# Gathering 1.1 million table rows: no two-SBUF operations on VectorE, one tile of each block by SyncE

## The chip, the core and the metric

The kernel runs on one core of a Trainium2 chip. A core has five engines that work side by side: TensorE (PE, matrix products, results in PSUM), VectorE (DVE), ScalarE (ACT), GpSimd (POOL) and SyncE (SP). In this kernel GpSimd issues the indirect DMAs, each of which fetches 128 rows of a table by 128 ids; SyncE issues ordinary DMAs. The metric is the time of one execution in device microseconds (us); smaller is better.

## What is computed

For each of 16384 samples there are 69 ids of one user and one label id, all rows of a table `emb` with 96 columns. Each user row is weighed by a small network that also sees the label's row, the weighted rows are summed in 10 groups of fields, and three dense layers give one number.

```python
u  = emb[batch_user]                       # 16384 x 69 x 96
ql = emb[batch_label[:, 0]]                # 16384 x 96
q  = broadcast(ql)
z  = concatenate([q, u, q - u, q * u])     # 384 wide
h  = dice(z @ W1 + b1, a1)                 # 64 wide
att = (h @ W2 + b2) @ W3 + b3              # 1 wide
pre = where(batch_user < ITEM_NUM, u * att, 0)    # ITEM_NUM = 100000
pooled = einsum('gf,bfe->bge', window, pre)       # 10 groups of fields
x = concatenate([pooled, ql])              # 1056 wide
h = dice(bn(x @ Wf1 + bf1), af1)           # 200 wide
h = dice(bn(h @ Wf2 + bf2), af2)           # 80 wide
out = h @ Wf3 + bf3
# bn(x) = x / sqrt(1 + eps);  dice(x, a) = (a * (1 - p) + p) * x,  p = sigmoid(bn(x))
```

## The kernel before

A block has 512 samples, and there are 32 blocks. The first 64 fields of a block form 64 "main chunks" of 512 rows (8 samples x 64 fields), the last 5 fields form 5 "tail chunks" (one field, 512 samples): 69 chunks, 276 gathers of 128 rows. Chunks are handled in pairs, one pair a step, 1104 steps in all, software-pipelined: a step gathers and turns pair i, computes the hidden layer of pair i-2 and pools pair i-8.

```python
def map_ids(n, ids):                       # ids of ITEM_NUM go to a row of zeros behind the table
    rows = ipool.tile([P, NT], I32, tag="rows", name=f"rows{n}")
    nc.vector.scalar_tensor_tensor(rows, ids[:, 0:NT], float(ITEM_NUM), ids[:, 0:NT],
                                   ALU.is_ge, ALU.add)                              # L110
    return rows

def head_gather(n, part):                  # 32 label rows of block n, by SyncE
    ...
    _, at = nc.values_load_multi_w_load_instructions(                               # L252
        lab[n : n + 1, part * NLD : (part + 1) * NLD],      # lab lies in HBM
        engines=[mybir.EngineType.SP], ...)
    for i, row in enumerate(at):
        nc.sync.dma_start(out=qs[n][p + i : p + i + 1, k, :], in_=emb[bass.ds(row, 1), :])  # L260

def fetch(i):                              # one pair of chunks
    ...
            for t in range(4):
                gather(u[:, 4 * j + t, :], rows[n][:, 4 * k + t : 4 * k + t + 1])   # L229, GpSimd
                nc.tensor.transpose(ptr[:, t * P : (t + 1) * P], u[:, 4 * j + t, :], ident)  # L325
    ...                                    # then q * u on VectorE (L328), a copy on ScalarE (L336)

def hidden(i, ph, uT, quT):                # four products into ph (L343), sigmoid, dice
    ...
    nc.vector.tensor_mul(y, ph, y)         # L347, ph in PSUM

def spread(b, row):                        # attention weights times the window of groups
    ...
    nc.vector.tensor_scalar(w, pt[...], bb, None, ALU.add)                          # L373
    nc.vector.tensor_tensor(rw..., R..., w..., ALU.mult)    # L376: R and w both in SBUF
    return rw

def pool(i, u, rw):                        # 4 products a chunk, two records each (L393)
    ...

def top1(n, h, part, p1):                  # first dense layer, 100 of its 200 outputs
    ...                                    # 16 products into p1, four in a step     L423
    nc.vector.tensor_scalar(x1, p1, S_BN, sbf1[h], ALU.mult, ALU.add)               # L427
    nc.scalar.activation(g1, x1, AF.Sigmoid, scale=S_DICE)
    nc.scalar.activation(g1, g1, AF.Identity, bias=af1c[h], scale=naf1c[h])
    nc.vector.tensor_mul(x1, x1, g1)       # L430: both in SBUF

def top2(n): ...                           # the same with 80 outputs; L438 and L441
def top3(n, x2): ...                       # one output; stored by SyncE at L449
```

The buffers `u` of the gathered rows are 14 pairs deep. In each block's 34.5 steps SyncE fetches 16 parts of 32 label rows for the block to come, the ids of a block (140 KB), and stores one block's results.

Of the kernel before, what the change touches and what calls it, by code (L numbers as in the profile page):

```python
# [53 lines left out]
NCOL = NT + NQ  # L54
NLD = 32
NPAIR = NBLK * NCH // 2
# [5 lines left out]


@with_exitstack
def rec_kernel(
# [3 lines left out]
    lab: bass.AP,  # L69
    emb: bass.AP,  # L70
    W1: bass.AP,
# [28 lines left out]
    xpool = ctx.enter_context(tc.tile_pool(name="xpool", bufs=1))  # L100

# [5 lines left out]
    def map_ids(n, ids):  # L107

        rows = ipool.tile([P, NT], I32, tag="rows", name=f"rows{n}")
        nc.vector.scalar_tensor_tensor(rows, ids[:, 0:NT], float(ITEM_NUM), ids[:, 0:NT], ALU.is_ge, ALU.add)  # L110
        return rows

    ids, rows = {0: load_ids(0)}, {}
    rows[0] = map_ids(0, ids[0])
# [74 lines left out]
    naf1c = [one_minus(t, f"naf1c{i}") for i, t in enumerate(af1c)]  # L189
    naf2c = one_minus(af2c, "naf2c")  # L190
    sbf1 = []
    for i in range(2):
        t = const.tile([DH, 1], F32, name=f"sbf1_{i}")
        nc.vector.tensor_scalar_mul(t, bf1c[i], S_BN)
        sbf1.append(t)
    sbf2 = const.tile([D2, 1], F32, name="sbf2")
    nc.vector.tensor_scalar_mul(sbf2, bf2c, S_BN)
# [30 lines left out]
    def gather(dst, index):  # L228
        nc.gpsimd.indirect_dma_start(  # L229
            out=dst,  # L230
            out_offset=None,
            in_=emb,
            in_offset=bass.IndirectOffsetOnAxis(ap=index, axis=0),
        )

    def chunk(c):

        return divmod(c, NCH)

    def first_head():  # L240

        q = bpool.tile([P, NQ, E], F32, tag="q", name="q0")
        for k in range(NQ):
            gather(q[:, k, :], ids[0][:, NT + k : NT + k + 1])
        return q

    def head_gather(n, part):

        if part == 0:
            qs[n] = bpool.tile([P, NQ, E], F32, tag="q", name=f"q{n}")  # L250
        k, p = divmod(part * NLD, P)
        _, at = nc.values_load_multi_w_load_instructions(  # L252
            lab[n : n + 1, part * NLD : (part + 1) * NLD],
            engines=[mybir.EngineType.SP],
            min_val=0,
            max_val=ITEM_NUM,
            skip_runtime_bounds_check_because="labels are rows of the table",
        )
        for i, row in enumerate(at):
            nc.sync.dma_start(out=qs[n][p + i : p + i + 1, k, :], in_=emb[bass.ds(row, 1), :])  # L260
# [31 lines left out]
    def seed(i):  # L292

        ph = ps_h.tile([P, 512], F32, tag="h", name=f"ph{i}")
        nc.tensor.matmul(ph, zrow[:, 0:P], zrow, start=True, stop=False)  # L295
        (n0, k0), (n1, k1) = chunk(2 * i), chunk(2 * i + 1)
        if n0 == n1 and k1 < NMAIN:
            nc.scalar.copy(  # L298
                ph.rearrange("h (s f) -> h s f", f=FM), by_field(cs[n0][0][:, k0 * NS : (k0 + 1) * NS])
            )  # L300
        elif n0 == n1 and k0 >= NMAIN:
            nc.scalar.copy(ph, cs[n0][1])
        else:
            for j, (n, k) in enumerate([(n0, k0), (n1, k1)]):
                lo, hi = j * H1, (j + 1) * H1
                if k < NMAIN:
                    nc.scalar.copy(
                        ph[lo:hi].rearrange("h (s f) -> h s f", f=FM),
                        by_field(cs[n][1][lo:hi, k * NS : (k + 1) * NS]),
                    )  # L310
                else:
                    nc.scalar.copy(ph[lo:hi], cs[n][1][lo:hi, :])
        return ph

    def fetch(i):

        u = upool.tile([P, 8, E], F32, tag="u", name=f"u{i}")
        uT = tpool.tile([E, 2, 512], F32, tag="uT", name=f"uT{i}")
        quT = tpool.tile([E, 2, 512], F32, tag="quT", name=f"quT{i}")
        for j in range(2):  # L320
            n, k = chunk(2 * i + j)
            ptr = ps_tr.tile([E, 512], F32, tag="tr", name=f"ptr{i}_{j}")
            for t in range(4):
                gather(u[:, 4 * j + t, :], rows[n][:, 4 * k + t : 4 * k + t + 1])
                nc.tensor.transpose(ptr[:, t * P : (t + 1) * P], u[:, 4 * j + t, :], ident)  # L325
            q = qTs[n % 2][0:E]
            if k < NMAIN:
                nc.vector.tensor_tensor(  # L328
                    quT[:, j, :].rearrange("e (s f) -> e s f", f=FM),
                    ptr.rearrange("e (s f) -> e s f", f=FM),  # L330
                    by_field(q[:, k * NS : (k + 1) * NS]),
                    ALU.mult,
                )
            else:
                nc.vector.tensor_tensor(quT[:, j, :], ptr, q[:, 0:BLK], ALU.mult)
            nc.scalar.copy(uT[:, j, :], ptr)  # L336
        return u, uT, quT
# [28 lines left out]
    def spread(b, row):  # L366

        pt = ps_x.tile([P, 4, 4, 32], F32, tag="x", name=f"patt{b}")
        for t in range(4):
            nc.tensor.transpose(pt[:, t].rearrange("p k j -> p (k j)"), row[:, t * P : (t + 1) * P], ident)  # L370
        rw = rpool.tile([P, 4, 2, 4, 2 * G], F32, tag="rw", name=f"rw{b}")
        w = rpool.tile([P, 4, 2, 4], F32, tag="w", name=f"w{b}")
        nc.vector.tensor_scalar(  # L373
            w, pt[:, :, :, 0:2].rearrange("p t k j -> p k j t"), bb, None, ALU.add
        )
        nc.vector.tensor_tensor(  # L376
            rw.rearrange("p k j t g -> p (k j t) g"),
            R.rearrange("p (k g) -> p k g", k=1).to_broadcast([P, 32, 2 * G]),
            w.rearrange("p k j (t o) -> p (k j t) o", o=1).to_broadcast([P, 32, 2 * G]),
            ALU.mult,  # L380
        )
        return rw

    def pool(i, u, rw):
# [6 lines left out]
        for j, n, k in todo:  # L391
            for t in range(4):
                nc.tensor.matmul(  # L393
                    pa[:, j, 2 * t : 2 * t + 2, :].rearrange("e n g -> e (n g)"),
                    u[:, 4 * j + t, :],
                    rw[:, i % 4, j, t, :],
# [14 lines left out]

    KTOP = G + 1 + NTAIL

    def top1(n, h, part, p1):

        if part == 0:
            p1 = ps_m.tile([DH, BLK], F32, tag="m", name=f"p1_{n}_{h}")
        for k in range(part * KTOP // 4, (part + 1) * KTOP // 4):
            if k <= G:
                w, x = wf1[:, k], pooled[n][:, k, :] if k < G else qTs[n % 2][0:E, 0:BLK]  # L420
            else:
                w, x = V[:, k - G - 1], pres[n][:, k - G - 1, :]
# [3 lines left out]
        x1, g1 = x1s[n][:, h, :], xpool.tile([DH, BLK], F32, tag="g1", name=f"g1_{n}_{h}")  # L426
        nc.vector.tensor_scalar(x1, p1, S_BN, sbf1[h], ALU.mult, ALU.add)  # L427
        nc.scalar.activation(g1, x1, AF.Sigmoid, scale=S_DICE)
        nc.scalar.activation(g1, g1, AF.Identity, bias=af1c[h], scale=naf1c[h])
        nc.vector.tensor_mul(x1, x1, g1)  # L430

    def top2(n):
        x2 = xpool.tile([D2, BLK], F32, tag="x2", name=f"x2_{n}")
        g2 = xpool.tile([DH, BLK], F32, tag="g1", name=f"g2_{n}")[0:D2]
        p2 = ps_m.tile([D2, BLK], F32, tag="m", name=f"p2_{n}")
        for i in range(2):
            nc.tensor.matmul(p2, wf2[:, i, :], x1s[n][:, i, :], start=(i == 0), stop=(i == 1))
        nc.vector.tensor_scalar(x2, p2, S_BN, sbf2, ALU.mult, ALU.add)  # L438
        nc.scalar.activation(g2, x2, AF.Sigmoid, scale=S_DICE)
        nc.scalar.activation(g2, g2, AF.Identity, bias=af2c, scale=naf2c)  # L440
        nc.vector.tensor_mul(x2, x2, g2)  # L441
        return x2

    def top3(n, x2):
        p3 = ps_m.tile([1, BLK], F32, tag="m", name=f"p3_{n}")
        nc.tensor.matmul(p3, wf3, x2, start=True, stop=True)
        res = xpool.tile([1, BLK], F32, tag="res", name=f"res{n}")
        nc.vector.tensor_scalar(res, p3, bf3c, None, ALU.add)
        nc.sync.dma_start(out=out_v[n : n + 1], in_=res)  # L449
# [3 lines left out]
    cs, pooled, pres, x1s, x2s, qs, us, hs, phs, ys, bands, rws, p1s = ({} for _ in range(13))  # L453

    def top_steps(n):


        def half(h, part):
            if h == 0 and part == 0:
                x1s[n] = xpool.tile([DH, 2, BLK], F32, tag="x1", name=f"x1_{n}")  # L460
            p1s[n] = top1(n, h, part, p1s.get(n))

        steps = [lambda h=h, part=part: half(h, part) for h in range(2) for part in range(4)]
        steps.append(lambda: x2s.__setitem__(n, top2(n)))
        steps.append(lambda: top3(n, x2s.pop(n)))
# [8 lines left out]
    for n in range(NBLK):  # L474
        first, end = n * NCH // 2, ((n + 1) * NCH - 1) // 2
        if n > 0:
            at(first - 24, lambda n=n: ids.__setitem__(n, load_ids(n)))
            at(first - 21, lambda n=n: rows.__setitem__(n, map_ids(n, ids[n])))
            for part in range(BLK // NLD):
                at(first - 31 + part, lambda n=n, part=part: head_gather(n, part))  # L480
            at(first - 11, lambda n=n: head_turn(n, qs.pop(n)))
            at(first - 9, lambda n=n: cs.__setitem__(n, head_row(n)))
        for s, work in enumerate(top_steps(n)):
            at(end + POOL_LAG + 4 + s, work)
# [3 lines left out]
    with tc.manual_schedule():  # L488
        head_turn(0, first_head())
        cs[0] = head_row(0)  # L490
        for i in range(NPAIR + POOL_LAG + 16):
            if 0 <= i - 1 < NPAIR:
                phs[i - 1] = seed(i - 1)
            if 0 <= i - POOL_LAG < NPAIR:
                k = i - POOL_LAG
                pool(k, us.pop(k), rws[k // 4])
                if k % 4 == 3:
                    rws.pop(k // 4)
# [14 lines left out]
            if 0 <= i - 2 < NPAIR:  # L513
                ys[i - 2] = hidden(i - 2, phs.pop(i - 2), *hs[i - 2])
            if i < NPAIR:
# [58 lines left out]
```

## Time and profile before

| | |
|---|---|
| time, median of 3 | 15474.4 us (15444.3 to 15497.4) |
| the profiled execution | 11178.9 us, span 11177.1 |
| PE busy | 9700.5 us (87%), granted clock 0.707 on average |
| ACT busy | 3760.0 us (34%) |
| DVE busy | 3187.3 us (29%) |
| POOL busy | 8404.8 us (75%) |
| DMA | 456.8 MB moved, 41 GB/s |

The profiled execution is shorter than the timed ones. All that a view of the profile says holds for the profiled execution.

How to read the views: a group's line gives source line, engine, operation, tiles (out<-in), the count, then busy time and the mean of one instruction in ns, then the idle time of the engine just before these instructions and what ended most of it. A line of the waits reads "engine, tile, line <- what it waited for: us in total, times, longest". "Issue" is idle time in which the engine waited for nothing that the profile shows. A line of the timeline begins with the start and the length in us. A row of digits cuts the span in 40 slices, in tenths of it; PEclk is the clock that was granted to TensorE.

### The profile page before, as it was taken

Reading aid. Unit: us, or ns where it says so; the run is one execution under the profiler, and the core shown is the slowest. Engines: PE = TensorE matmul, PEld = TensorE weight load, DVE = VectorE, ACT = ScalarE, POOL = GpSimd, SP = SyncE. Lnnn points to the kernel's source line nnn. Section 1 sums busy time; section 2 is a strip of 40 time slices with the busy share of each in tenths; the row PEclk is TensorE's granted clock in tenths of the full one; section 3 lists DMA queues with packets and bytes.
Section 4 is the critical chain, followed back from the end, with each engine's and each line's share of the span. In section 5 each row is a group of like instructions: output and inputs, shape, how many; then the busy total and the mean of one; then the engine's idle time right before and its main releaser. Section 6 shows DMA issues by size and latency. Waiting matters only on the chain.

```text
span 11177.1 us, 157529 instructions
## 1 busy us (share of the span) xinstructions
PE 9700.5 (87%) x41348; PEld 4721.0 (42%) x41348; DVE 3187.3 (29%) x5424; ACT 3760.0 (34%) x6086; POOL 8404.8 (75%) x8842
## 2 busy tenths in 40 slices
PE   6888888888888898888888888888888888988888
PEld 3444444444444444444444444444444344444444
DVE  2222222222222222222222222222222222222222
ACT  2333333333333333333333333333333333333332
POOL 7777777777777777777777777777777777777775
PEclk6767677677776767767777667776677776677767
DMA  2222222222222222222222222222222222222221
GB/s 45 41 41 41 41 41 41 41 41 41 41 41 41 41 41 41 41 42 41 41 41 41 41 41 41 40 41 42 41 41 41 41 42 41 41 41 41 41 40 29
DMA packets 323169, 456.81 MB, mean 41 GB/s; under 512 B 175712, under 2 KB 180864, under 8 KB 322272
## 3 DMA queue, kind: packets, MB, share of 16 engines
q0 software_dynamic: 282752, 434.87, 19.6%
q1 hardware_dynamic: 37886, 10.92, 0.5%
q8 instruction: 333, 5.46, 0.2%
q14 instruction: 564, 4.62, 0.1%
q10 hardware_dynamic: 1634, 0.94, 0.0%
HBM read 446.04 MB, written 0.07 MB: 40 GB/s over the span
## 4 chain that ended last, share of the span: by engine, by line
PE 33%; POOL 32%; issue 16%; DMA 10%; SPq 5%; ACT 2%; DVE 1%; POOLq 0%; ACTq 0%
POOL u L229 32%; PE ph L343 12%; DMA u<-in_emb,rows 10%; PE acc L393 9%; PE p L423 4%; SPq L260 3%; PE ptr L325 3%; PE prow L354 2%; SPq L252 2%; PE ph L295 2%; PE pa L363 1%; ACT y L346 1%; DVE y L347 1%; ACT y L345 1%; PE patt L370 1%
## 5 line engine op out<-in xcount | busy, mean ns | idle before, releaser
L229 POOL DMA_INDIRECT u<-in_emb,rows x8832 | 8400.1, 951 | 2692.9 <-issue 2459.0
L325 PE MATMUL ptr<-ident,u 128*96 128x128 f32 x8832 | 2006.4, 353 | 1189.5 <-DMA u<-in_emb,rows 1172.1
L325 PEld LDWEIGHTS ptr<-ident,u 128*96 128x96 f32 x8832 | 1221.0, 155 | 3053.7 <-DMA u<-in_emb,rows 1526.9
L393 PEld LDWEIGHTS acc<-rw,u 128*96 128x96 f32 x16384 | 2048.5, 217 | 531.8 <-issue 531.2
L393 PE MATMUL acc<-rw,u 128*96 128x20 f32 x16384 | 2160.4, 282 | 1.8 <-DVE rw L376 1.3
L336 ACT COPY uT<-ptr 96x512 f32<-96x512 f32 x2208 | 1283.4, 581 | 2207.0 <-DVE quT L328 2039.4
L347 DVE TENSOR_TENSOR y<-ph,y 128x512 f32<-128x512 f32 x1104 | 763.5, 692 | 4394.8 <-ACT y L346 4292.3
L345 ACT ACTIVATE y<-ph 128x512 f32<-128x512 f32 x1104 | 659.1, 597 | 3754.1 <-PE ph L343 3753.9
L343 PE MATMUL ph<-uT,A 96*64 96x512 f32 x4416 | 1793.5, 904 | 0.0
L343 PE MATMUL ph<-quT,w 96*64 96x512 f32 x4416 | 1671.9, 847 | 0.0
L328 DVE TENSOR_TENSOR quT<-ptr,qT 96x512 f32<-96x512 f32 x2048 | 1348.9, 679 | 611.5 <-PE ptr L325 607.0
L402 DVE COPY pooled<-acc 96x160 f32<-96x160 f32 x1008 | 433.3, 430 | 2189.9 <-PE acc L393 2184.4
L346 ACT ACTIVATE y<-y,a1c,na1c 128x512 f32<-128x512 f32 x1104 | 897.2, 813 | 36.6
L343 PEld LDWEIGHTS ph<-quT,w 96*64 96x64 f32 x4416 | 442.8, 194 | 1074.9 <-issue 1074.9
L298 ACT COPY ph<-cT 128x512 f32<-128x512 f32 x1008 | 591.3, 587 | 498.2 <-PE ph L295 497.8
L295 PE MATMUL ph<-zrow 1*128 1x512 bf16 x1104 | 527.6, 478 | 193.4 <-DVE y L347 191.7
L423 PE MATMUL p<-pooled,wf 96*100 96x512 f32 x1280 | 659.4, 660 | 1.2 <-DVE x L427 0.8
L343 PEld LDWEIGHTS ph<-uT,A 96*64 96x64 f32 x4416 | 282.6, 177 | 550.0 <-issue 464.8
L354 PE MATMUL prow<-y,v 128*32 128x512 f32 x2208 | 455.2, 909 | 0.0
L356 ACT COPY row<-prow 128x512 f32<-128x512 f32 x276 | 161.5, 585 | 628.4 <-PE prow L354 622.9
L423 PEld LDWEIGHTS p<-pooled,wf 96*100 96x100 f32 x1280 | 232.2, 190 | 287.7 <-issue 285.5
L423 PE MATMUL p<-pre,V 96*100 96x512 f32 x640 | 314.6, 625 | 0.0
(71 smaller groups left out, 2318.5 us busy)
## 6 DMA issues: line engine op xcount, KB each, us to landing
q<-in_emb SPq DMA_DIRECT2D x15872, 0.4 KB
u<-in_emb,rows POOLq DMA_INDIRECT x8832
ids<-in_idx SPq DMA_DIRECT2D x32, 140.0 KB
wf<-in_Wf ACTq DMA_DIRECT2D x1, 825.0 KB
out<-res SPq DMA_DIRECT2D x32, 2.0 KB
w<-in_W SPq DMA_DIRECT2D x1, 96.0 KB
q<-in_emb,ids POOLq DMA_INDIRECT x4
wf<-in_Wf ACTq DMA_DIRECT2D x1, 62.5 KB
```

Of the source, the lines that this page charges most:

```text
L229: nc.gpsimd.indirect_dma_start(out=dst, out_offset=None, in_=emb, in_offset=bass.IndirectOffsetOnAxis(ap=index, axis=0),)
L295: nc.tensor.matmul(ph, zrow[:, 0:P], zrow, start=True, stop=False)
L325: nc.tensor.transpose(ptr[:, t * P : (t + 1) * P], u[:, 4 * j + t, :], ident)
L328: nc.vector.tensor_tensor(quT[:, j, :].rearrange("e (s f) -> e s f", f=FM), ptr.rearrange("e (s f) -> e s f", f=FM), by_field(q[:, k * NS ...
L336: nc.scalar.copy(uT[:, j, :], ptr)
L343: nc.tensor.matmul(ph[j * H1 : (j + 1) * H1, :], w, x[:, j, :], start=False, stop=last)
L345: nc.scalar.activation(y, ph, AF.Sigmoid, scale=S_DICE)
L346: nc.scalar.activation(y, y, AF.Identity, bias=a1c, scale=na1c)
L347: nc.vector.tensor_mul(y, ph, y)
L354: nc.tensor.matmul(pr[32 * k : 32 * (k + 1), :], v2, y, start=True, stop=True)
L393: nc.tensor.matmul(pa[:, j, 2 * t : 2 * t + 2, :].rearrange("e n g -> e (n g)"), u[:, 4 * j + t, :], rw[:, i % 4, j, t, :], start=True, st ...
L423: nc.tensor.matmul(p1, w[:, h * DH : (h + 1) * DH], x, start=(k == 0), stop=(k == KTOP - 1))
```

## The change

It has four parts:

- **No VectorE operation with two SBUF inputs.** The product with the window takes its weights from PSUM at once, in two operations instead of an addition and a product. The dense layers' dice does its scaling inside the sigmoid and multiplies straight from PSUM. The mapping of ids goes: the table of user rows is now one of its own, `rows`, whose last row is zero, so the ids are used as they are.
- **The last block in halves.** Its five tail chunks are taken before its last 16 main chunks, so that the dense layers of the first 256 samples can run before the last rows are there. Four poolings move one step earlier at the end.
- **Ids for SyncE's registers from SBUF.** They are loaded into a tile once per block, and registers are filled from it, instead of from HBM.
- **One more tile of rows per block through SyncE.** The first 128 rows of main chunk 8 (`SOLO`) of each block but the first come row by row from SyncE, like the labels, and not by a gather.

It is for GpSimd, which issues all gathers: one gather fewer in each block, and no VectorE operation with two SBUF inputs beside the others; for SyncE, which takes the tile over; and for the end of the run. The core of the diff:

```diff
+PARTS = P // NLD
+SOLO = 4 * 8
+EARLY = 3 * NMAIN // 4
...
-    rows[0] = map_ids(0, ids[0])
...
     def chunk(c):
-        return divmod(c, NCH)
+        n, k = divmod(c, NCH)
+        if n == NBLK - 1 and k >= EARLY:
+            k = NMAIN + k - EARLY if k < EARLY + NTAIL else k - NTAIL
+        return n, k
...
+    def load_solo(n):
+        t = spool.tile([(NQ + 1) * PARTS, NLD], I32, tag="sid", name=f"sid{n}")
+        nc.sync.dma_start(out=t, in_=solo[n : n + 1].rearrange("o p n -> (o p) n"))
+        return t
...
         _, at = nc.values_load_multi_w_load_instructions(
-            lab[n : n + 1, part * NLD : (part + 1) * NLD],
+            index,                                  # a row of the tile of load_solo
...
+    def solo_part(n, part):                         # parts 0-15: labels, 16-19: the solo tile
...
+                if n > 0 and 4 * k + t == SOLO:
+                    tiles.append(solos.pop(n))
+                else:
+                    tiles.append(u[:, 4 * j + t, :])
+                    gather(rows, tiles[-1], ids[n][:, 4 * k + t : 4 * k + t + 1])
...
-        nc.vector.tensor_scalar(w, pt[:, :, :, 0:2]..., bb, None, ALU.add)
-        nc.vector.tensor_tensor(rw..., R..., w..., ALU.mult)
+        for j in range(2):
+            nc.vector.scalar_tensor_tensor(rw[:, :, j, :], pt...[:, :, j : j + 1]..., bb, R...,
+                                           ALU.add, ALU.mult)
...
+    def dice(x, g, p, b, weights):
+        sb, sa, sna = weights
+        nc.scalar.activation(g, p, AF.Sigmoid, bias=sb, scale=S_BN * S_DICE)
+        nc.scalar.activation(g, g, AF.Identity, bias=sa, scale=sna)
+        nc.vector.scalar_tensor_tensor(x, p, b, g, ALU.add, ALU.mult)
...
-            for part in range(BLK // NLD):
-                at(first - 31 + part, lambda n=n, part=part: head_gather(n, part))
+            at(first - 33, lambda n=n: sids.__setitem__(n, load_solo(n)))
+            for part in range((NQ + 1) * PARTS):
+                at(first - 32 + part, lambda n=n, part=part: solo_part(n, part))
...
+        else:                                       # the last block
+            for s, work in enumerate(top_steps(n, slice(0, BLK // 2))):
+                at(NPAIR - 7 + s, work)
+            for s, work in enumerate(top_steps(n, slice(BLK // 2, BLK))):
+                at(end + POOL_LAG + 1 + s, work)
...
-        "emb": np.concatenate([x["emb"], np.zeros((1, E), np.float32)], axis=0),
+        "emb": x["emb"],
+        "rows": np.concatenate([x["emb"][:ITEM_NUM], np.zeros((1, E), np.float32)], axis=0),
```

## The prediction

> **What bounds the kernel now.** I read the engine totals first, then GpSimd's groups and waits, then single gathers. GpSimd does nothing but gathers, and its row shows how it spends the run:
>
> ```profile
> POOL 7777777777777777777777777777777777777775
> PEclk6767677677776767767777667776677776677767
> ...
> L229 POOL DMA_INDIRECT u<-in_emb,rows x8832 | 8400.1, 951 | 2692.9 <-issue 2459.0
> ...
> POOL u L229 <- issue: 2459.0, 8065, 0.3
> ...
> POOL u L229 <- PE ptr L325: 105.8, 347, 0.3
> ```
>
> GpSimd is 75% busy in every slice, and what is missing is not waiting. It stands idle 8065 times "for issue", 2459.0 us in total, which is 0.305 us each time and never over 0.3 as rounded. Waits put down to other engines have the same 0.3 as their longest, so they are that same gap under another name. The list of gather starts has no real hole anywhere: a gather of 128 rows begins every 1.249 us (0.944 by the median of one, 0.305 between two). With the 4 gathers of the first labels, 8836 x 1.249 = 11036 us; the first starts at 3.4 us and the last ends at 11101.3 us. So **the whole profiled span is one string of gathers**, with 62 us over, and a tail of 75.8 us behind the last.
>
> The other engines wait for it:
>
> ```profile
> PE ptr L325 <- DMA u<-in_emb,rows: 1172.1, 1424, 2.7
> ...
> SPq L449 <- DVE res L448: 2230.6, 31, 350.3
> ...
> 2006.70 13.11 SPq L260 DMA_DIRECT2D q<-in_emb  x32
> ```
>
> TensorE has 87% busy but waits 1172 us for gathered rows. SyncE, which fetches label rows one DMA each, waits 2230.6 us at the stores of results, so it has slack too: 20%.
>
> The 62 us over: the mean gather takes 951 ns, the median 944, so the total is 8400.1 - 8832 x 0.944 = 62.7 us too long. It is not spread evenly. Gathers of 1.2 to 1.6 us lie where VectorE works on two SBUF inputs:
>
> ```profile
> 11097.48 0.94 POOL L229 DMA_INDIRECT u<-in_emb,rows  x1 [0.30 <-issue]
> ...
> 11098.42 0.82 DVE L376 TENSOR_TENSOR rw<-R,w 128x640 f32<-128x640 f32 x1
> ...
> 11098.73 1.33 POOL L229 DMA_INDIRECT u<-in_emb,rows  x1 [0.30 <-issue]
> ...
> 11100.36 0.94 POOL L229 DMA_INDIRECT u<-in_emb,rows  x1 [0.30 <-issue]
> ```
>
> The product `rw = R * w` runs from 11098.42 to 11099.24; the gather that begins inside it takes 1.33 instead of 0.94 us. Pairing every gather over 0.96 us with what VectorE does in its time leaves only 5 without such a partner. By line, the excess over 0.943 us is 48.2 us for L376, 18.3 for L430, 2.3 for L441, 1.9 for L110 and 3.5 for the tail weights at the start.
>
> **The page and the times disagree.** The profiled execution took 11179 us, the timed ones 15474. No row of the page explains 4.3 ms. This is the largest uncertainty here, and I come back to it.
>
> [...]
>
> **The change, part by part, in the profiled execution.**
>
> 1. *One tile per block through SyncE.* Blocks 1 to 31 give up one gather each: 31 x 1.249 = **-39 us**. For this SyncE takes 20 parts of 32 rows per block instead of 16. A part costs 13.1 us of issues plus 4.9 us of register load (1.1 pointer, 3.4 values, 0.4 between), 18.0 us, so 16 parts take 288 of the 344 us that a block's 275 gathers last. With 20 parts at 18.0 it would be 360 us, and SyncE would set the pace.
> 2. *Ids from SBUF.* That is why this part is there. [...] SyncE stays under 344[...]. The solo tile is read some 15 steps (150 us) after its last row is issued. Also the first turned labels, for which TensorE waits 46 us once near the start, come earlier; GpSimd didn't feel that wait, so it is worth nothing.
> 3. *No two-SBUF operations.* The excess of L376, L430, L441 and L110 goes: 48.2 + 18.3 + 2.3 + 1.9 = 70.7 us; the tail weights keep theirs. Against the median instead of 0.943 it is some 8 us less. I take **-65 us**. What comes in instead reads PSUM as one input. VectorE loses 72 us (L427 and L438) it wasn't short of. ScalarE reads PSUM in the sigmoid at the same size, and the one PSUM buffer of the top layers is held about 2 us longer, in steps of 10 us; nothing on the path.
> 4. *Last block in halves.* After the last gather the chain now shows:
>
> ```profile
> 11132.79 17.26 PE p L423 x32
> 11150.08 0.76 DVE x L427
> 11150.88 13.99 PE p L423 x32
> ```
>
>    Half of the columns is done before the end: 31.3 us of products become about 15. The layers behind them (11164.9 to 11177.1) shrink by some 3 us with 256 columns. Before 11132.8 the last gather is followed by 8 pairs' poolings and the tail fields; four poolings of 1.5 to 2.8 us and two or three attention rows of 2 us move ahead of it: 8 to 12 us. Together **-30 us**, a tail of about 46.
>
> Sum: -39 - 65 - 30 = -134 us, a profiled span of about 11,043.
>
> **From there to the timed run.** Two readings. If the 4.3 ms are something that both kernels carry, the gain stays 134 us: 15,340. If the gathers themselves are slower when timed, (15474 - 76)/8836 = 1.743 us each, the first part grows to 31 x 1.743 = 54 us, the lock's to between 65 and 65 x 1.4 = 91, the tail's to 30 to 40: 150 to 185 us, or 15,290 to 15,325. I choose **15,325 us**, 1.0% less.
>
> **Rivals.**
>
> *SyncE becomes the bound.* For: it is the next busiest, with 128 more rows a block, 25%. If the timed run is slow because of SyncE, that is 483 us a block and 30 us a part instead of 18; were it the row issues, 20 such parts with a short load would take about 550 us a block, 17.6 ms. Against: its waits for results show 72 us of slack a block, and a row's data packet begins 0.85 us after its issue while eight semaphores in turn allow 8 x 0.41 = 3.3 us. If the slow thing were the register loads from HBM, the change would remove it and gain milliseconds. I give each of these 7 to 8%.
>
> *TensorE is the bound when timed.* With the clock at half throughout, start-to-start times in half-clock stretches add up to 10.7 us a pair of chunks, x 1104 = 11.8 ms. That is over 11.1 but far from 15.5, so the clock would have to be lower still than anything the profile shows. Then only the tail counts: 15,430.
>
> *The additional table costs.* The rows are now in HBM twice, 38 MB each. If the 4.3 ms had to do with the size of the inputs (44 MB before), the change would add nearly as much again, 19 ms. Nothing in the page speaks for it; 3%.
>
> *The lock is dearer than it looks.* All operations removed last 228.4 + 44.6 + 22.0 + 14.0 = 309 us. If a timed gather were held for the whole of each, 2% would be gained.
>
> **Range and chances.** The parts that I trust give 15,290 to 15,340; TensorE as the bound 15,430; the dearer lock 15,150. The range is 15,120 to 15,500, with the SyncE and table cases outside. 2% below is 15,165, 2% above 15,784. Faster by over 2%: 0.12 (dear lock, register loads). Slower by over 2%: 0.11 (SyncE, table). Within: 0.77.
>
> **What will show it.** Right: 8805 gathers at 1.249 us with no holes; gathers over 1.2 us nearly gone but for the first 150 us; last gather near 10,997; a tail of 40 to 50 us; SyncE still waiting at the store of results; register loads under 3 us. Wrong: GpSimd waiting for TensorE or for a solo tile (SyncE too slow), long gathers that stay beside PSUM operations (then it was not the second SBUF input), or a timed gain far from the profiled 134 us, which would mean that the two executions have different bounds.

## The result: 7.5% slower, and the profile after

The changed kernel took 16634.7 us (median of 4 runs, 16599.8 to 16664.8) against 15467.8 us before (median of 4, 15444.3 to 15497.4): a ratio of 1.0753, 95% interval 1.0721 to 1.0784. Predicted were 15,325 us and a range up to 15,500.

This time the page belongs to the times: the profiled execution of the changed kernel took 16615 us, and its span is 16613.2. First GpSimd's digits and group from the page of the changed kernel:

```profile
POOL 5444455444554445444455454554445544455444
...
L232 POOL DMA_INDIRECT u<-in_rows,ids x8801 | 8324.3, 946 | 8157.6 <-PE acc L416 4266.0
```

A gather takes 946 ns, as before (951), and there are the 31 fewer. But GpSimd is 50% busy instead of 75. It stands idle 8157.6 us, and what ends most of that is no longer "issue" but a product of TensorE (`acc`, the pooling, which gives a buffer of gathered rows free). Who holds TensorE, and what SyncE waits for, is in the waits of the changed kernel (us in total, times, longest):

```profile
POOL u L232 <- PE acc L416: 4266.0, 247, 104.6
...
PE pq L284 <- DMA q<-in_emb: 2918.1, 62, 62.2
...
SPq L473 <- DVE res L472: 485.7, 3, 284.5
```

TensorE waits 62 times, twice a block, for the label rows, which SyncE fetches. In the page of before the same wait was small:

```profile
PE pq L265 <- DMA q<-in_emb: 50.3, 24, 46.4
```

SyncE's wait at the stores of results has fallen from 2230.6 us in 31 stores to 485.7 in 3: in the other blocks SyncE comes to the store late. So the order of waiting has turned round: GpSimd waits for TensorE, TensorE for label rows, and SyncE for almost nothing. **SyncE sets the pace.**

Why it is so slow shows when its issues are laid beside what GpSimd does. Two stretches of the changed kernel's SyncE timeline (start, length, number of row issues; register loads are inside), and then the busy time by windows for the same stretches, whose pairs are PE, PEld, DVE, ACT and POOL:

```profile
1979.89 60.06 SPq L269 DMA_DIRECT2D q<-in_emb  x123
...
2098.81 78.56 SPq L269 DMA_DIRECT2D solo<-in_rows  x64
```

```profile
1980.00:2040.00 60.00, 0.42 (x1) 0.16 (x1) 0.00 (x0) 0.00 (x0) 0.00 (x0) 0.50 0.01 1
2099.00:2177.00 78.00, 46.79 (x193) 26.61 (x193) 13.13 (x24) 16.58 (x28) 50.59 (x55) 0.54 0.16 35
```

While GpSimd stands still (the fifth pair, 0.00 us), SyncE issues 123 rows in 60.06 us, 0.49 us each. Beside 55 gathers it needs 78.56 us for 64: 1.23 us each. Taken from one register load to the next, a part of 32 rows has a median of 15.6 us where no gather begins (157 parts) and of 30.3 us where gathers, at 1.249 us each, fill 80 to 95% of it (237 parts); the mean of all is 26.0 us. 20 such parts are 520 us a block, and 31 blocks 16.1 ms. In the page of before, a part cost 18.0 us beside gathers.

Where GpSimd stands, the other engines mostly stand too, so they could be what slows SyncE. The same trace tells them apart. Taken in groups of 8 rows without a register load between them, it has 98 groups in which no gather begins and TensorE begins at least one product a us: 0.41 us a row (median), as in the 497 groups where neither works. In 53 groups gathers begin and no product does: 1.09 us a row. SyncE's slowness goes with the gathers, not with TensorE.

### The profile page after: what moved, and what is told of

Same layout as the page of the kernel before. It is cut to its first block, busy times and chain, and to the rows that moved or that the text cites. A ratio compares the mean times of both kernels' runs of the same rounds, so it can differ in the third digit from the quotient of the medians.

```text
span 16613.2 us, 169743 instructions
## 1 busy us (share of the span) xinstructions
PE 9769.2 (59%) x41418; PEld 4967.8 (30%) x41418; DVE 3034.8 (18%) x5303; ACT 3745.8 (23%) x6092; POOL 8329.0 (50%) x8811
## 5 line engine op out<-in xcount | busy, mean ns | idle before, releaser
L232 POOL DMA_INDIRECT u<-in_rows,ids x8801 | 8324.3, 946 | 8157.6 <-PE acc L416 4266.0
L416 PEld LDWEIGHTS acc<-rw,u 128*96 128x96 f32 x16322 | 2147.8, 227 | 3562.8 <-issue 3556.7
L416 PE MATMUL acc<-rw,u 128*96 128x20 f32 x16322 | 2261.0, 290 | 4.3 <-DVE pooled L425 3.7
L367 PE MATMUL ph<-uT,A 96*64 96x512 f32 x4416 | 1877.8, 939 | 5.6 <-issue 5.4
L349 PE MATMUL ptr<-ident,u 128*96 128x128 f32 x8801 | 1713.3, 354 | 174.2 <-issue 140.3
L349 PEld LDWEIGHTS ptr<-ident,u 128*96 128x96 f32 x8801 | 1285.8, 164 | 1671.5 <-issue 1506.2
L367 PE MATMUL ph<-quT,w 96*64 96x512 f32 x4416 | 1782.0, 895 | 2.0 <-issue 1.8
L284 PE MATMUL pq<-ident,q 128*96 128x128 f32 x128 | 42.6, 381 | 2918.3 <-DMA q<-in_emb 2918.1
L453 PE MATMUL p<-pooled,wf 96*100 96x512 f32 (+1 forms) x1320 | 638.6, 621 | 21.7 <-issue 17.7
```

The lines of the kernel that those rows point to most:

```text
L232: nc.gpsimd.indirect_dma_start(out=dst, out_offset=None, in_=table, in_offset=bass.IndirectOffsetOnAxis(ap=index, axis=0),)
L349: nc.tensor.transpose(ptr[:, t * P : (t + 1) * P], tiles[-1], ident)
L367: nc.tensor.matmul(ph[j * H1 : (j + 1) * H1, :], w, x[:, j, :], start=False, stop=last)
L416: nc.tensor.matmul(pa[:, j, 2 * t : 2 * t + 2, :].rearrange("e n g -> e (n g)"), u[4 * j + t], rw[:, 4 * t + i % 4, j, :], start=True, sto ...
L453: nc.tensor.matmul(p1, w[:, h * DH : (h + 1) * DH], x, start=(k == 0), stop=(k == KTOP - 1))
```

## The experiments

They were run on seven chips, which showed two kinds of behaviour. On five of them the kernel before takes 11.2 ms, as in its page; on two it takes 15.7 ms, near its times. I call them chips of the first and of the second kind. No chip was used at two different times, so whether the kind belongs to the chip or to the time is not shown. Each comparison is with the kernel before on the same chip. Nothing in a kernel chose the chip.

| run | kind of chip | this, us | before there, us |
|---|---|---|---|
| before_again | 1 | 11211 | 11204 |
| after_no_solo | 1 | 11127 | 11204 |
| after_gather_labels | 1 | 11282 | 11204 |
| before_gather_labels | 1 | 11359 | 11204 |
| after_again | 1 | 11070 | 11184 |
| after_hbm_ids | 1 | 11568 | 11184 |
| after_two_sp | 1 | 11184 | 11184 |
| no_solo_2 | 2 | 15107 | 15748 |
| after_three_sp | 2 | 14158 | 15748 |
| gather_labels_2 | 2 | 13597 | 15748 |
| gather_fewer_records_3 | 2 | 13564 | 15733 |

The theory after the first profile: SyncE's rows set the pace of both kernels in the timed runs, and the solo tile adds a quarter to them. Rivals: the gathers themselves are slower when timed; or one of the new forms on VectorE slows the changed kernel.

### The first four: fewer rows for SyncE

**before_again**: no edit.

> Theory (SyncE sets the pace): in the executions that take 15.5 ms SyncE issues its label rows about half as fast as in the profiled execution of before, some 30 us for a part of 32 rows instead of 18, so that 16 parts fill a block of 483 us; its wait for the results, 2230 us before, falls under 500 us and GpSimd shows waits for buffers that TensorE holds. Rival (the gathers are slower): SyncE keeps its slack and a gather comes every 1.74 us instead of 1.249. Rival (it was another state of the chip): 11.2 ms again.

11211 us: the chip was of the first kind, and its trace is like the page of before. It shows that the page of before was no accident; that its 15.5 ms were none either is seen further down, where it takes 15.7 ms.

**after_no_solo**: the changed kernel without the solo tile.

```diff
-SOLO = 4 * 8
+SOLO = -1
...
-            for part in range((NQ + 1) * PARTS):
+            for part in range(NQ * PARTS):
```

> The changed kernel without the solo tile: 16 parts of rows for SyncE instead of 20. SyncE sets the pace: 16 parts of 26 us are 416 us a block, 13.3 ms, below both kernels. Rival (the new form of spread or dice is what slows the changed kernel): 16.5 ms as before, since a gather more per block changes 40 us.

11127 us, ratio 0.993 (0.991 to 0.995). On this chip neither number could come out, as SyncE isn't the bound there: it waits 3211.9 us in 33 stores for results.

**after_gather_labels**: SyncE issues no rows at all.

```diff
-            at(first - 33, lambda n=n: sids.__setitem__(n, load_solo(n)))
-            for part in range((NQ + 1) * PARTS):
-                at(first - 32 + part, lambda n=n, part=part: solo_part(n, part))
+            for k in range(NQ):        # gather(emb, qs[n][:, k, :], ids[n][:, NT + k : NT + k + 1])
+                at(first - 20 + k, lambda n=n, k=k: head_gather(n, k))
```

> The changed kernel with labels and solo tile fetched by GpSimd, SyncE issuing no rows at all. SyncE sets the pace: it is gone, and GpSimd's 8832 + 128 gathers at 1.249 us set it: 11,191 + 3 + a tail of 45 = 11,240 us. Rival (slower gathers): 8960 x 1.743 = 15,620 us. Rival (new forms of spread and dice): 15,600 or more.

11282 us, ratio 1.0068 (1.0052 to 1.0085). Expected were 11,240; the tail is 66.5 us instead of 45, which is half of the difference.

**before_gather_labels**: the same edit in the kernel before.

> The kernel before with its labels fetched by GpSimd. SyncE sets the pace: 8960 gathers at 1.249 us, 63 us of lock, a tail of 76: 11,335 us, that is 95 us above the changed kernel with the same gathers, which would be the worth of the two-SBUF part and of the halves alone. Rival (slower gathers): 15,690 us.

11359 us, ratio 1.0136 (1.0119 to 1.0153). Between this run and the last lie the parts on VectorE and on the last block, on one chip: 77 us by the medians, where 95 were expected. The row of the gathers (min/median/max in ns) shows the two-SBUF operations leaving, first in before_gather_labels, then in after_gather_labels:

```profile
L229 POOL DMA_INDIRECT u<-in_emb,rows x8832: 941/947/1594, 8.6 to 11282.6; - x197
```

```profile
L232 POOL DMA_INDIRECT u<-in_rows,ids x8832: 940/944/1073, 8.5 to 11188.3; - x197
```

No gather over 1.1 us is left. In these two traces, which are 108 us apart, the last one starts 94 us earlier, more than the 65 expected, partly because the median is 3 ns lower here, which over 8960 gathers is 27 us.

### The changed kernel where SyncE is quick

**after_again**: no edit.

> The changed kernel again, since the kernel before took 15.5 ms at one time and 11.2 at another. Theory (what slows SyncE in the slow executions belongs to the chip on which a kernel runs, not to the change): where the kernel before takes 11.2 ms, SyncE needs 32 x 0.408 + 2.2 = 15.3 us a part, 20 parts are 305 of 343 us, GpSimd sets the pace and the changed kernel takes 8805 x 1.250 + 3 + a tail of 67 = 11,075 us; where the kernel before takes 15.5 ms it takes 16.6. Rival (the solo tile alone makes SyncE stall, on any chip): 16.6 ms in both cases.

11070 us, ratio 0.9899 (0.9883 to 0.9916). The same program that loses 7.5% gains 1% on a chip of the first kind. after_again_2, the same on another chip, had 0.9903. From after_again's trace: SyncE's waits, its moves (min/median/max) and its issues beside gathers.

```profile
SPq L473 <- DVE res L472: 1322.0, 31, 315.9
```

```profile
L269 SPq MOVE q<-in_emb x15872: 29/29/38, 15.2 to 10467.9; - x199
```

```profile
2059.79 43.61 SPq L269 DMA_DIRECT2D q<-in_emb  x94
```

The same line of the changed kernel's recorded profile:

```profile
L269 SPq MOVE q<-in_emb x15872: 1/29/1412, 15.1 to 16015.3; - x199
```

A register move, which the trace records apart from the row's DMA, takes 29 to 38 ns here and up to 1412 there; the register operations beside it (FUSED_REGOPS) take 37 to 51 here and up to 1412 there. So it is not only the row DMAs that are slow there, and the length that comes up most is about 0.7 us (of 2363 moves over 0.1 us, 1651 last 0.68 to 0.72). Here 94 rows beside running gathers take 43.61 us, 0.46 each, a part 15.6 us, and 1322 us of slack are left.

**after_hbm_ids**: registers loaded from HBM.

```diff
-        fetch_rows(table, dst[...], sids[n][part : part + 1, :])
+        fetch_rows(table, dst[...], solo[n, part : part + 1, :])
```

> The changed kernel with the ids for SyncE's registers loaded from HBM as before. A part costs 18.0 us, 20 parts 360 us against 343 us of gathers: where the kernel before takes 11.2 ms SyncE becomes the bound and the time is 31 x 360 + some 350 = 11,500 us, 4% over the changed kernel. Rival (the loads lie beside other work): as the changed kernel. Where the kernel before takes 15.5 ms: 20/16 of it, 19 ms.

11568 us, ratio 1.0344 (1.0289 to 1.0399). This makes SyncE the bound on a chip of the first kind. The chain's shares by engine, and the waits of the three engines concerned:

```profile
SPq 59%; issue 19%; PE 16%; ACT 3%; POOL 2%; DVE 1%; DMA 1%; ACTq 0%; POOLq 0%
```

```profile
POOL u L232 <- PE acc L416: 456.6, 77, 21.5
...
PE pq L284 <- DMA q<-in_emb: 2050.8, 52, 71.7
...
SPq L473 <- DVE res L472: 388.0, 3, 194.8
```

It is the picture of the changed kernel's recorded profile: three waits at the stores in place of 31, label rows late, GpSimd behind TensorE. The loads from SBUF are worth 500 us in this place (11568 against 11070), and without them 20 parts don't fit.

**after_two_sp**: half of the labels by SyncE, the other half and the solo tile by gathers.

```diff
+            for part in range(HSP * PARTS):        # HSP = 2
+                at(first - 32 + part, lambda n=n, part=part: solo_part(n, part))
+            for k in range(HSP, NQ):
+                at(first - 20 + k, lambda n=n, k=k: head_gather(n, k))
```

> The changed kernel with half of the labels by SyncE (8 parts a block) and the other half and the solo tile by gathers. SyncE needs 8 x 15.3 = 122 us a block at its fast pace and 8 x 26 = 208 us at the slow one, so GpSimd's 8832 + 4 + 62 = 8898 gathers set the pace wherever it runs: 8898 x 1.250 + 70 = 11,190 us. Rival (SyncE's slow pace also slows the gathers, or any part of rows is late): 13 ms or more where the kernel before takes 15.5.

11184 us, ratio 1.000 (0.9991 to 1.0008): 31 x 3 gathers more than the changed kernel, 116 us by their cadence and 114 measured. It did not fall on a chip of the second kind, so what it does there was not seen.

### On a chip of the second kind

**no_solo_2**: as after_no_solo.

> The same kernel as after_no_solo, to be read where the kernel before takes 15.5 ms, if this run falls on such a place. There a part beside running gathers takes SyncE 30 us in the changed kernel's slow profile and 15.6 us while GpSimd stands; 16 parts at a mixture of 26 are 416 us a block: 13.3 ms. Rival (SyncE slows down so far that the gathers stop, whatever the number of parts): 15.5 ms and more. Where the kernel before takes 11.2 ms: 11,127 again.

15107 us, ratio 0.960 (0.9525 to 0.9678). Against the kernel before, the changed one without its solo tile gains 4%; with it, it lost 7.5%. **The solo tile is what turned the change round**: 1.0753/0.9601 = 1.12. The two ratios come from different times, and the 1.0753 was measured once: after_again_2, which was to repeat it, fell on a chip of the first kind. But the 13.3 ms were wrong. A part takes 29.2 us on average, not 26, because with 16 parts GpSimd stands still for less of the time (no gather begins in 49 of 495 parts, against 157 of 619), and SyncE is quick only then (15.6 us a part against 30.3 in the changed kernel's recorded profile): 16 x 29.2 = 467 us a block, x 31 = 14.5 ms. SyncE still sets the pace:

```profile
SPq L473 <- DVE res L472: 592.8, 3, 399.2
```

**after_three_sp**: as after_two_sp with HSP = 3.

> Three label tiles of four by SyncE (12 parts a block), the fourth and the solo tile by gathers. GpSimd: 8832 + 4 + 31 = 8867 gathers x 1.250 + 70 = 11,155 us where the kernel before takes 11.2 ms. Where it takes 15.5: 12 parts of 30 us are 360 us against 345 us of gathers, so SyncE and GpSimd are about even: 11.2 to 11.7 ms. Rival there (slow as before): 15 ms.

14158 us, ratio 0.900 (0.892 to 0.908). SyncE's waits at the stores are 1526 us in 17 stores, so it no longer is the only bound, but the time is far above 11.7 ms. Something else is slow as well.

**gather_labels_2**: as after_gather_labels.

> The same kernel as after_gather_labels. SyncE issues no rows, so its time doesn't depend on SyncE's pace: 11,280 us wherever it runs, also where the kernel before takes 15.5 ms. Rival (there the gathers or something else are slow too): 13 ms or more in that place.

13597 us, ratio 0.864 (0.857 to 0.872). Both theory and rival were half right. Against no_solo_2, on the same chip, SyncE's rows cost 1.5 ms; against the kernel before, from which it differs in the other parts too, this run gains 2.1 ms. It still takes 2.3 ms more than on the first kind. Where these lie is seen in one step of gather_labels_2, in the timeline:

```profile
3009.73 1.03 PE L373 MATMUL ph<-quT,w 96*64 96x512 f32 x4
...
3010.69 1.08 PE L355 MATMUL ptr<-ident,u 128*96 128x128 f32 x8
...
3020.76 0.60 ACT L375 ACTIVATE y<-ph 128x512 f32<-128x512 f32 x1 [11.46 <-remote]
3021.39 0.81 ACT L376 ACTIVATE y<-y,a1c,na1c 128x512 f32<-128x512 f32 x1
3022.23 0.69 DVE L377 TENSOR_TENSOR y<-ph,y 128x512 f32<-128x512 f32 x1 [9.56 <-ACT y L376]
```

The hidden products end at 3010.76 by the trace, which works the end of a product out and does not record it. ScalarE's sigmoid, which waits for them, begins at 3020.76, ten microseconds later; "remote" means that the trace has no source for the signal. VectorE follows ScalarE 0.03 us later. The same on the first kind, in after_gather_labels:

```profile
3009.96 1.03 PE L373 MATMUL ph<-quT,w 96*64 96x512 f32 x4
...
3011.04 0.60 ACT L375 ACTIVATE y<-ph 128x512 f32<-128x512 f32 x1 [2.12 <-PE ph L373]
```

Over all 1104 steps the sigmoid starts a median of 47 ns behind the last hidden product there, and never over 51 ns in 99 of 100. In gather_labels_2 the median is 779 ns and a quarter are over 4.2 us. VectorE's product starts a median of 32 to 33 ns behind ScalarE in both. So of these two, the one that waits for TensorE is late, and the one that waits for ScalarE isn't.

This lateness goes with the gathers as well. In gather_labels_2, where no gather began in the 5 us before the products' end (38 steps), the sigmoid starts a median of 47 ns behind them, as on the first kind; where four began (605 steps), the median is 3.5 us. In after_gather_labels four began before 1100 of the 1104 products, and it is 47 ns. So on the second kind both SyncE and what waits for TensorE are late where gathers run. That is read from the traces; no run changed the gathers alone.

### Does it follow the number of instructions?

TensorE and SyncE have the most instructions in the changed kernel (85,648 and 60,514 in its recorded profile, where the next, GpSimd, has 9,932), and both are concerned; I tried whether it is their number.

**gather_more_records** and **gather_fewer_records**, from after_gather_labels:

```diff
+            for r in range(20):                             # gather_more_records, each step
+                nc.vector.memset(idle[:, r : r + 1], 0.0)
```

```diff
-            for t in range(4):                              # gather_fewer_records
-                nc.tensor.matmul(pa[:, j, 2 * t : 2 * t + 2, :]..., u[4 * j + t],
-                                 rw[:, 4 * t + i % 4, j, :], ...)
+            nc.tensor.matmul(pa[:, j]..., u[4 * j], rw...[:, i % 4, j], ...)
```

The second leaves out the pooling of three tiles of four.

> The kernel after_gather_labels with 20 writes of one number a step by VectorE, 22,080 small instructions that nothing waits for. Where the kernel before takes 11.2 ms: 11,280 still, as VectorE has room (28% busy). Where it takes 15.5: if it is the number of instructions on the core that counts, 22,080 more of 109,062 add up to 20%: 14.5 to 16 ms; if only TensorE's own instructions count, 13.6 ms as without them.

11263 us on the first kind, 1.0073 (1.005 to 1.0096) of before: harmless there, as expected. It did not fall on the second kind.

> The kernel after_gather_labels with one pooling product of 80 columns a chunk in place of four of 20, all with the first tile's rows: it leaves out the pooling of three tiles of four, and TensorE has 24,576 fewer instructions of 82,836. Where the kernel before takes 11.2 ms: GpSimd sets the pace, 11,260. Where it takes 15.5: if TensorE's lateness follows the number of its instructions, 11.5 to 12.3 ms instead of 13.6; if it doesn't, 13.3 or more.

11248 us on the first kind, 1.0057 (1.0034 to 1.008), and 11246 as gather_fewer_records_2 on another such chip.

> As gather_fewer_records: three of four poolings left out, 24,576 of TensorE's 82,836 instructions fewer. Where the kernel before takes 15.5 ms: if TensorE's lateness follows the number of its instructions, 11.5 to 12.3 ms instead of 13.6; if it doesn't, 13.3 or more. Elsewhere 11,250 again.

This one fell on the second kind: 13564 us, ratio 0.862 (0.856 to 0.867), within 0.3% of gather_labels_2's. With 30% fewer instructions of TensorE the sigmoid starts a median of 1.56 us behind the product, not sooner. That theory falls. The pair also settles another rival, a lower TensorE clock on the second kind: this kernel was granted 0.685 to 0.688 on the first kind and 0.674 to 0.681 here, nearly the same, and takes 2.3 ms more.

### Runs that missed the second kind

after_again_2 (11071 us against 11182) and three further runs of the kernel before fell where that takes 11.2 ms:

> The kernel before, to be read where it takes 15.5 ms. SyncE sets the pace: a part of 32 rows takes 30 us or a little more, SyncE waits for results under 600 us in all instead of 2230, and TensorE waits for the label rows (q) for 1 ms or more. Rival (TensorE's lateness sets the pace and SyncE has slack): SyncE's wait stays over 2000 us. Elsewhere 11,180 again.

11185 us, and 11184 and 11182 in before_again_2 and before_again_3. So the kernel before has no trace where it takes 15.5 ms, and that SyncE bounds it there too is worked out, not seen: 16 parts at the 29.2 us of no_solo_2 and 2.4 us more for loading from HBM are 506 us a block, x 31 = 15.7 ms, with 15,748 measured on that chip. That it comes so close is partly luck: the same sum falls 0.5 ms short of the changed kernel (16.1 against 16.6) and 0.6 short of no_solo_2 (14.5 against 15.1).

## Why the prediction was wrong, point by point

- *GpSimd bounds the kernel, 1.249 us a gather.* True of the page and of every chip of the first kind; not of the times. The page could not tell, but the 4.3 ms between page and times said that the times were of something else.
- *One tile through SyncE, -39 us; SyncE stays under 344 us.* **This is the step that failed.** On the first kind it held: 15.6 us a part, 312 us a block, 1322 us of slack. In the timed runs a part cost 26.0 us on average, 30.3 beside gathers, and 20 of them 520 us a block: SyncE set the pace, and GpSimd, which was to gain 39 us from it, stood idle for 8157.6 us. The pace of a part in the page of before, 0.41 us a row beside gathers, held on the first kind (0.46, register loads included) and not here (1.23). The sign of being wrong that the prediction names for this, GpSimd waiting for TensorE, is what the profile shows.
- *From there to the timed run.* Both readings that I chose between, a load common to both kernels and slower gathers, left SyncE as it was in the page. The gathers are not slower (946 ns).
- *The rival "SyncE becomes the bound".* It was the right one, with 30 us a part before and 17.6 ms after against 16.6 measured: too high, since SyncE is quick again (15.6 us a part) whenever GpSimd has to stop, which its lateness itself brings about. It was given 7 to 8%.
- *Ids from SBUF.* Right: 2.2 us a load in after_again instead of 4.9, where under 3 was predicted. No load in the page of before came from SBUF, so the length was my estimate. Without this part the change loses on the first kind too (after_hbm_ids, 1.034).
- *No two-SBUF operations, -65 us.* Right on the first kind: the last gather ends at 10997.7 us in after_again and at 11101.3 in the page of before, 104 us apart, of which 39 are the 31 gathers. With the second SBUF input gone, the longest gather falls from 1594 to 1073 ns (before_gather_labels, after_gather_labels). "The lock" in the prediction stands for these longer gathers; the traces show their length beside such operations, not what causes it.
- *The halves, -30 us.* Direction right, size wrong. The tail is 66.6 us in after_again, 75.8 in the page: -9. The products are 19.7 us instead of 15, and part of the first half has slid behind the last gather:

```profile
11008.23 3.39 PE p L453 x8
...
11013.81 1.90 PE p L453 x8
...
11034.60 9.21 PE p L453 x32
...
11045.51 10.54 PE p L453 x32
```

  These pieces of after_again's chain of waits lie between the last gather's end at 10997.7 and 11056.1. Steps in program order that were meant to hide under gathers came after them.
- *The sum.* A span of 11,043 was predicted where the page's conditions hold, and 11,064 measured. All but the tail was sized well, for the first kind; the timed runs were not of it.

What stays open: why, where gathers run, SyncE is slow in the changed kernel's recorded profile (1.23 us a row against 0.49) and the successors of TensorE are late in gather_labels_2 (3.5 us against 0.047). It was not the number of TensorE's instructions. One suspect is the recording of the profile itself. For one program, after_gather_labels and gather_labels_2, the trace holds 168,542 signals of semaphores on the first kind and 54,744 on the second, so two thirds of these records are missing there. And of the 19,842 register moves of SyncE in the changed kernel's recorded profile, 5366 last under 20 ns by the trace, while in after_again none lasts under 29, which suggests that some start times were taken late. This makes the suspicion stronger; since all these runs are recorded, it can't be settled from them, nor whether a run without recording would be slow at all.

## What to carry to other kernels

When a page and the times disagree by a quarter, find out first which engine could differ, above all the one next to the bound: here SyncE of the changed kernel had 1322 us of slack in one execution (after_again) and set the pace in another (485.7 us in 3 stores). Work moved off the bound to a second engine must fit at that engine's worst pace beside the first (here 30.3 us a part), not at the pace of one page (15.6 in after_again). On chips of the first kind the changed kernel is the quickest of all that were run (0.990 of before); on those of the second kind the one without rows by SyncE beats both, 13,597 us and 0.864, and costs 0.7% on the others, so, as far as these recorded runs tell, it is the one to keep where the chip isn't known.

## What the runs showed of the hardware that was not expected

- The kernel before takes 11,170 to 11,211 us on five chips and 15,679 to 15,789 on two others.
- In the changed kernel's recorded profile a register move of SyncE takes up to 1.4 us, in after_again 0.04 at most, and a row takes 1.09 us (median) where gathers begin and no product does, 0.41 where no gather begins.
- On a chip of the second kind (gather_labels_2), ScalarE starts a median of 0.8 us and up to 43 us behind the product it waits for (0.047 us in after_gather_labels, and in gather_labels_2 too where no gather began in the 5 us before), while VectorE behind ScalarE keeps its 0.033 us (median).
- A load of 32 registers takes 2.1 us (median) from SBUF in the changed kernel's recorded profile; in the page of before it takes 3.4 from HBM, plus 1.1 for the pointer.
